# The passage from layer 0 to layer 1 of a two-layer kernel: a sum of expert results on TensorE, layer norm scaled by ScalarE, copies of early attention on ScalarE, and token numbers computed ahead of row numbers

## The chip, the cores and the metric

The kernel runs on one NeuronCore of a Trainium2 chip. The metric is the time of one execution on the device in microseconds (us); the kernel before has a median of 1236.36 us over 3 runs (1234.08 to 1241.92). The engines are called by the names of the profile: PE (TensorE), DVE (VectorE), ACT (ScalarE), POOL (GpSimd) and SP (SyncE, which issues most transfers).

## The reference

Two layers act on 16 x 256 = 4096 tokens of 128 channels in float32. Each layer is a layer norm, a mixer of tokens `s`, an expert network `g`, and a gated sum back into `x`:

```python
x = L0_attn_x
xn = _layernorm(x)
s = _L0_attn_ref(xn, ...)          # gated linear attention, 4 heads, chunks of 64
g = _silu(_L0_ffn_ref(xn, ...))    # 8 experts, the best 2 for each token, weighted
x = x + s * g
xn = _layernorm(x)
s = _L1_attn_ref(xn, ...)          # causal softmax attention, 16 heads of 8 channels
g = _silu(_L1_ffn_ref(xn, ...))    # 16 experts, the best 2, weighted; then an RMS norm
x = x + s * g
```

The change touches the end of layer 0 (`silu` of the two expert results of each token, times `s`, added to `x`), the second layer norm, the routing to experts of both layers, and some copies in the first steps of layer 1's attention.

## The kernel before, in words

**Tiling.** The tokens are 8 blocks of 512 (`BT`), each a tile of 128 partitions x 4 x 128. `xs[b]` holds a block of x, `xns[b]` its norm (the first 128 columns of the tile `xnx`), `xnTs[b]` the transpose of the norm; `s_sbs[b]` is the same memory, taken later for the mixer's result.

**Stages.** Layer 0 starts with norm and routing. Then its experts (`experts0`) run interleaved with its mixer (`gated`, which yields pieces of `decays(b)` and `mixed(b)`). After the last expert, the passage begins: the rest of the mixer for blocks 6 and 7 is interleaved with `combined(b)`, one generator for each block. Then layer 1's attention starts, in pieces, interleaved first with the last steps of `combined` and with layer 1's routing (`route`, lay = 1), later with layer 1's experts (`experts`).

**`combined(b)`** works in four steps. (1) `results` (L439) has SP read both expert results of each token from the DRAM tensor `yd` into the tile `gg` (L444); DVE adds them into `acc` (L767); ACT makes the sigmoid with three activations (L769 to L771); DVE multiplies `acc` by `s` in place (L772). (2) DVE multiplies by the sigmoid (L774), adds into `xs[b]` (L775) and takes mean and variance (L213, L214); ACT makes `rs = exp(-0.5 ln(var + eps))` (L216, L217). (3) DVE scales and shifts x into `xn` in four instructions (L221); PE transposes each quarter (L224); ACT copies the transpose out of PSUM (L225). (4) PE makes the router's logits (L779) and DVE adds their bias (L780). `staged` (L197) starts one block in each tick and moves every live block by one step, oldest first; so a tick holds step 4 of block b-3, step 3 of b-2, step 2 of b-1 and step 1 of b, and then one piece of the mixer. The PSUM tiles of these steps come from the pool `c_ps` of two buffers: L816 while the mixer runs, `pf_` (L1212) after.

**`route`** finds each token's two experts, writes the weighted rows of the norm to DRAM (L285), gives every (token, expert) pair a place in a slot of 128 rows, and inverts this map with one-hot matmuls: in eight rounds DVE makes `ohp` and `hi` (L342, L345), ACT makes `lo` (L346), DVE scales `hi` (L349) and PE adds into `pT` (L351). Then follow the rows for empty slots (L357 to L362), a `yield`, and the copy `tb` of `pT` on ACT (L365) with `row`, `seconds`, `toks` and `rows` on DVE (L367 to L370). At each `yield` of layer 1's route one attention piece is put in (`fill(1)`, L1243). `toks` gives the gather its addresses, `rows` the scatter its own.

**What sets the order.** The passage stands in `manual_schedule` for ACT, PE, DVE and SP: on these, instructions run in the order in which the program makes them. POOL's gathers (`slot_in`, L377) and scatters (`slot_out`, L389) are further ordered by `pooled` and by two helpers: `passed(inst)` (L400) notes an instruction, and `behind(inst)` (L404) makes a transfer wait for the last one that was noted:

```python
def passed(inst):
    reached[:] = [inst.ins.name]

def behind(inst):
    for name in reached:
        tc.add_manual_dep(inst.ins, name, SYNC, reason="spread over other work")
```

After layer 1's route all rows of the first expert batch are gathered at once: `fetch(len(wanted))`, L1248.

**Attention pieces.** `setup(b)` makes kT, qT and v (L886 to L902): `k_part` copies by ACT (L890) and masks by DVE (L892), `q_part` copies qT out of PSUM by DVE (L884). For each tile of 128 queries, scores Sq (L923) give maxima on DVE (L933, L935), `queries` (L985 to L991) makes the shifted queries, scores Sk (L956) go through exponentials on ACT (L963), `weighted` makes `yx` (L1006), DVE copies it to `yt` (L1011), and `normed` transposes (L1018) and divides it into `y` (L1026, L1028). DVE instructions collected in `later` are issued at the next piece. `pS`, `ps` and `pf_` (L1210 to L1212) have two PSUM buffers each.

Of the kernel before, what the change touches and what calls it, by code (L numbers as in the profile page):

```python
# [10 lines left out]
F32 = mybir.dt.float32  # L11
I32 = mybir.dt.int32
BF16 = mybir.dt.bfloat16
AF = mybir.ActivationFunctionType
ALU = mybir.AluOpType
# [43 lines left out]
def two_layer_kernel(  # L59
# [146 lines left out]

    def normed_T(pool, ps, b):

# [7 lines left out]
        nc.scalar.activation(rs, mv[:, :, 1], AF.Ln, bias=eps5)  # L216
        nc.scalar.activation(rs, rs, AF.Exp, scale=-0.5)  # L217
        yield
        pt = ps[0].tile([P, NTL, P], F32, tag=ps[1], name="ptn")
        for t in range(NTL):  # L220
            nc.vector.tensor_scalar(  # L221
                xn[:, t, :], xb[:, t, :], mv[:, t, 0:1], rs[:, t : t + 1], ALU.subtract, ALU.mult
            )
            nc.tensor.transpose(pt[:, t, :], xn[:, t, :], ident)  # L224
# [21 lines left out]
    def route(pool, ps, sc, ne, slt, lay, emap, rm, ptag, tkw):  # L246
# [91 lines left out]
        for c in range(2):  # L338
            for n0 in range(0, NT32, NH):
# [10 lines left out]
                for n in range(NH):  # L350
# [3 lines left out]
                    )  # L354
                yield

        nc.vector.scalar_tensor_tensor(base, cnt, 2.0 * 4096 - 0.5, base, ALU.add, ALU.add)  # L357
# [4 lines left out]
        nc.vector.tensor_tensor(em, em, slotno[:, :slt], ALU.mult)  # L362
        yield
        tb = pool.tile([P, 2, slt], F32, tag="rt_tb", name="tb")
        nc.scalar.copy(tb, pT)  # L365
        row, tok = tb[:, 0, :], tb[:, 1, :]
        nc.vector.scalar_tensor_tensor(row, row, float(P), tok, ALU.mult, ALU.add)  # L367
        nc.vector.tensor_scalar(seconds[lay], row, 4096.0, None, ALU.is_ge)
        nc.vector.scalar_tensor_tensor(toks[lay], seconds[lay], -4096.0, row, ALU.mult, ALU.add)
        nc.vector.tensor_tensor(rows[lay], row, em, ALU.add)  # L370
# [29 lines left out]
    def passed(inst):  # L400

        reached[:] = [inst.ins.name]
# [76 lines left out]
    with ExitStack() as cg:  # L479
# [283 lines left out]
        def combined(b):  # L763

            gg = results(cmb, 0, b)
            acc = cmb.tile([P, NTL, D], F32, tag="acc", name="acc")
            nc.vector.tensor_tensor(acc, gg[:, 0], gg[:, 1], ALU.add)  # L767
            sl = cmb.tile([P, NTL, D], F32, tag="sl", name="sl")
            nc.scalar.activation(sl, acc, AF.Exp, scale=-1.0)  # L769
            nc.scalar.activation(sl, sl, AF.Ln, bias=1.0)  # L770
            nc.scalar.activation(sl, sl, AF.Exp, scale=-1.0)  # L771
            nc.vector.tensor_tensor(acc, acc, s_sbs[b], ALU.mult)  # L772
            yield
            nc.vector.tensor_tensor(sl, sl, acc, ALU.mult)  # L774
            nc.vector.tensor_tensor(xs[b], xs[b], sl, ALU.add)  # L775
            yield from normed_T(cmb, c_ps, b)
            pl = c_ps[0].tile([P, NTL, E1], F32, tag=c_ps[1], name="plg1")
# [47 lines left out]
    with ExitStack() as c1:  # L825
# [41 lines left out]
        def attention():  # L867
# [5 lines left out]
            def setup(b):  # L873
# [6 lines left out]
                def q_part(i):  # L880
                    pq = ps.tile([P, BT], F32, tag="ps", name="pq1")
                    nc.tensor.matmul(pq, wqs[i], xnT, start=True, stop=True)
                    qT[i] = wk_.tile([P, BT], F32, tag=f"qT{i}", name=f"qT{i}")
                    passed(nc.vector.tensor_copy(qT[i], pq))  # L884

# [110 lines left out]
            def weighted(i):  # L996
# [13 lines left out]
                yt = yxs[i] = wk_.tile([P, 4, P], F32, tag="yt", name="yt")  # L1010
                later.append(lambda: passed(nc.vector.tensor_copy(yt, yx)))  # L1011

# [199 lines left out]
        pf_ = c1.enter_context(tc.tile_pool(name="l1pf", bufs=2, space=PSUM))  # L1212
        pieces, ahead, later, done = attention(), [], [], set()

# [20 lines left out]
        with tc.manual_schedule(engines={ET.Activation, ET.PE, ET.DVE, ET.SP}):  # L1235
# [5 lines left out]
            with tc.tile_pool(name="rt1", bufs=1) as rt1:  # L1241
                for _ in route(rt1, pf_, sc1, E1, SLT, 1, emap1, starts(rt1, E1), "pf", {"tag": "pf"}):
                    fill(1)  # L1243
            ccmb.close()
            hp = c1.enter_context(tc.tile_pool(name="l1h", bufs=2))
            batches = [(j0, min(CPB, SLT - j0)) for j0 in range(0, SLT, CPB)]
# [69 lines left out]
```

## Time and profile before

| | us |
|---|---|
| median of 3 runs | 1236.36 |
| lowest and highest run | 1234.08, 1241.92 |
| profiled execution, its own time | 1251.36 |
| its span, first to last instruction | 1249.6 |
| first read of `gg` in the passage (L444) | at 471.9 |
| first DVE sum of results (L767) | at 475.8 |
| mixer of layer 0 done (copy of block 7, L651) | at 564.9 |
| routing of layer 1 begins (L236) | at 591.8 |
| first gather of layer 1 (L377) | at 676.2 |

The profile is one execution. A row of the timeline gives start in the span and duration in us, engine, line of the code, operation, tile written and tiles read, their shape and type, and how many instructions were merged; the bracket at the end is the time for which the engine stood idle before, and the instruction or transfer that released it. A matmul of float32 is two instructions (passes) on PE, so "x4" is two calls. The table of windows gives the busy time of each engine in a stretch, with the number of instructions in parentheses; PEclk is the clock granted to PE as a share of the full one. PEld is the loading of weights into PE, which overlaps its matmuls.

### The profile page before, as it was taken

The numbers are of one execution on the slowest core, as the hardware profiler recorded it, in microseconds if no ns is written. First come the engines' busy times: TensorE is split into PE (matmuls) and PEld (weight loads), VectorE is DVE, ScalarE is ACT, GpSimd is POOL, SyncE is SP. The second block draws the span as 40 slices with busy tenths as digits, with TensorE's granted clock in tenths as the row PEclk, the third lists the DMA queues.
The fourth block names the chain that finished last, engine by engine and source line by source line (L and its number), as shares of the span: only waits on it lengthen the run. The fifth ranks groups of instructions, "written<-read, shape, count | busy, mean of one in ns | idle before, by whom it ended". The sixth has DMA issues, their size and how long they took to land. (4 is left out here: it accounts for less than half of the span.)

```text
span 1249.6 us, 17774 instructions
## 1 busy us (share of the span) xinstructions
PE 910.2 (73%) x6394; PEld 646.3 (52%) x6394; DVE 769.5 (62%) x1442; ACT 588.7 (47%) x1059; POOL 390.2 (31%) x422
## 2 busy tenths in 40 slices
PE   6756478878787773767374887878897889888673
PEld 4334256666566652554142565566565656665342
DVE  5675455646455546736886655756765766675853
ACT  3331267665657462431131455544454655544643
POOL 2000235454455320000103333633652553443120
PEclk9967689899889885677777887988988989899776
DMA  4040248842333202100403030431331333122211
GB/s 112 1 69 1 64 107 211 165 111 72 97 99 106 62 15 88 51 1 1 69 1 129 20 119 18 136 116 33 124 125 48 100 129 117 25 94 66 84 35 34
DMA packets 88415, 95.41 MB, mean 76 GB/s; under 512 B 22228, under 2 KB 64040, under 8 KB 88328
## 3 DMA queue, kind: packets, MB, share of 16 engines
q1 hardware_dynamic: 78632, 74.32, 21.9%
q0 software_dynamic: 9696, 19.97, 6.1%
q8 instruction: 50, 0.82, 0.3%
q14 instruction: 37, 0.30, 0.1%
HBM read 78.03 MB, written 22.51 MB: 80 GB/s over the span
## 5 line engine op out<-in xcount | busy, mean ns | idle before, releaser
L389 POOL DMA_INDIRECT yd<-og,row x150 | 153.8, 1025 | 240.9 <-DVE og L758 116.6
L377 POOL DMA_INDIRECT xg<-xnd,tok x150 | 148.9, 993 | 155.0 <-DVE yT L646 79.7
L956 PE MATMUL Sk<-qm,kT 32*128 32x256 f32 x768 | 129.1, 460 | 43.3 <-ACT pr L963 20.5
L966 POOL TENSOR_SCALAR_AFFINE_SELECT pr<-pr 128x1024 f32<-128x1024 f32 x64 | 72.0, 1125 | 275.7 <-ACT pr L963 275.3
L963 ACT ACTIVATE pr<-Sk 128x1024 f32<-128x1024 f32 x96 | 97.8, 1019 | 96.9 <-PE Sk L956 94.6
L923 PE MATMUL Sq<-km,qT 32*128 32x256 f32 x768 | 132.6, 457 | 12.1 <-DVE mx L933 4.3
L956 PEld LDWEIGHTS Sk<-qm,kT 32*128 32x128 f32 x768 | 76.2, 214 | 61.7 <-ACT pr L963 29.3
L923 PEld LDWEIGHTS Sq<-km,qT 32*128 32x128 f32 x768 | 70.2, 207 | 58.2 <-issue 35.3
L935 DVE TENSOR_REDUCE negm<-Sq 128x8 f32<-128x1024 f32 x64 | 78.0, 1219 | 30.3 <-PE Sk L956 21.7
L721 PEld LDWEIGHTS pf<-xgT,wt 128*128 128x128 f32 x568 | 77.2, 208 | 31.4 <-issue 15.0
L721 PE MATMUL pf<-xgT,wt 128*128 128x128 f32 x568 | 82.9, 294 | 12.0 <-ACT sg L730 6.3
L726 ACT ACTIVATE sg<-pf,nb 128x128 f32<-128x128 f32 x142 | 44.1, 361 | 62.1 <-PE pf L721 61.2
L737 DVE SCALAR_TENSOR_TENSOR gt<-pf,nb,sg 128x128 f32<-128x128 f32 x142 | 42.8, 344 | 47.1 <-ACT sg L730 47.0
L546 PE MATMUL pq<-xnT,sb_wq 128*128 128x512 f32 x64 | 45.4, 850 | 30.0 <-DVE sp L519 28.5
L917 PE MATMUL Sq<-mq,identb 128*128 128x512 bf16 x128 | 42.0, 412 | 16.7 <-DVE negm L935 10.6
L1129 DVE SCALAR_TENSOR_TENSOR z<-pf,z 128x512 f32<-128x512 f32 (+1 forms) x40 | 27.1, 678 | 43.5 <-ACT z L1127 43.5
L1125 ACT ACTIVATE z<-pf 128x512 f32<-128x512 f32 (+1 forms) x40 | 23.7, 593 | 60.9 <-PE pf L1121 60.9
L1173 PE MATMUL pe<-wt,th 128*128 128x128 f32 x316 | 46.7, 309 | 7.0 <-DVE th L1164 7.0
L1173 PEld LDWEIGHTS pe<-wt,th 128*128 128x128 f32 x316 | 43.4, 220 | 14.0 <-issue 10.9
L754 PE MATMUL pe<-sb_wo,gt 128*128 128x128 f32 x284 | 40.1, 300 | 13.0 <-ACT xgT L700 13.0
L754 PEld LDWEIGHTS pe<-sb_wo,gt 128*128 128x128 f32 x284 | 37.2, 210 | 21.5 <-ACT xgT L700 18.1
L351 PE MATMUL pT<-ohj,ohp 128*128 128x142 bf16 (+1 forms) x128 | 14.7, 275 | 45.4 <-DVE ohj L349 45.4
(269 smaller groups left out, 2114.1 us busy)
## 6 DMA issues: line engine op xcount, KB each, us to landing
wt<-bank SPq DMA_DIRECT2D x79, 385.0 KB
wt<-in_w_dram SPq DMA_DIRECT2D x71, 256.0 KB
gg<-yd SPq DMA_DIRECT2D x32, 256.0 KB
xnd<-xnx SPq DMA_DIRECT2D x16, 260.0 KB
xg<-xnd,tok POOLq DMA_INDIRECT x150, 3.4
yd<-og,row POOLq DMA_INDIRECT x150, 2.5
x<-in_x_dram SPq DMA_DIRECT2D x8, 256.0 KB
bank<-in_freq_dram SPq DMA_DIRECT2D x1, 2048.0 KB
```

The lines of the kernel that those rows point to most:

```text
L377: return nc.gpsimd.indirect_dma_start(out=xg[:, i, :], out_offset=None, in_=xnds[lay], in_offset=bass.IndirectOffsetOnAxis(ap=toks[lay][:, ...
L389: give = nc.gpsimd.indirect_dma_start(out=yds[lay], out_offset=bass.IndirectOffsetOnAxis(ap=rows[lay][:, j : j + 1], axis=0), in_=og[:, i, ...
L546: nc.tensor.matmul(pq[:, c], w_[:, h * DK : (h + 1) * DK], xnT, start=True, stop=True)
L721: nc.tensor.matmul(pf[:, c, :], wts[i][:, c * P : (c + 1) * P], xgT[:, i, :], start=True, stop=True)
L726: nc.scalar.activation(sg[:, c, :], pf[:, 2 + c, :], AF.Exp, scale=-1.0, bias=nbs[i][:, 2 + c : 3 + c])
L754: nc.tensor.matmul(pe[:, i, :], gts[i][:, c, :], sb_wo0[:, c, :], start=(c == 0), stop=(c == 1))
L923: nc.tensor.matmul(S[:, c, js, :], qT[part][r, tq], km[r, js, tk], start=not diag, stop=True, skip_group_check=True,)
L935: passed(nc.vector.tensor_reduce(ng, S, AX.X, ALU.max, negate=True))
L956: nc.tensor.matmul(S[:, c, js, :], kT[part][r, tk], qm[r, js, :], start=True, stop=True, skip_group_check=True,)
L963: nc.scalar.activation(pr, S, AF.Exp, scale=scale)
L966: pooled(nc.gpsimd.affine_select(pr_, pr_, pattern=[[0, 8], [1, P]], compare_op=ALU.is_ge, fill=0.0, base=0, channel_multiplier=-1,))
L1173: nc.tensor.matmul(pe[:, i - i0, :], ths[i // 2][:, 2 * (i % 2) + c, :], wts[i][:, 2 * H1 + c * D : 2 * H1 + (c + 1) * D], start=(c == 0), ...
```

## The change

It has four parts. The sum of both results is made by two accumulating matmuls with the identity into a PSUM tile `both`, which ACT and DVE then read. The layer norm of layer 1 alone is scaled by ACT, as `x * rs + nb`, where a new small DVE instruction makes `nb = -mean * rs` behind the statistics. While `early` holds (from the start of layer 1's attention to the end of layer 1's routing), qT and yt are copied by ACT, and these copies are not marked `passed`. In `route` of both layers, `tb`, `row`, `seconds` and `toks` come one `yield` earlier, ahead of the work for empty slots; `rows` stays at the end.

```diff
-    def normed_T(pool, ps, b):
+    def normed_T(pool, ps, b, on_act=False):
...
         nc.scalar.activation(rs, rs, AF.Exp, scale=-0.5)
+        if on_act:
+            nb = pool.tile([P, NTL], F32, tag="nb", name="nb", bufs=3)
+            nc.vector.scalar_tensor_tensor(nb, mv[:, :, 0], -1.0, rs, ALU.mult, ALU.mult)
         yield
         pt = ps[0].tile([P, NTL, P], F32, tag=ps[1], name="ptn")
         for t in range(NTL):
-            nc.vector.tensor_scalar(
-                xn[:, t, :], xb[:, t, :], mv[:, t, 0:1], rs[:, t : t + 1], ALU.subtract, ALU.mult
-            )
+            if on_act:
+                nc.scalar.activation(
+                    xn[:, t, :], xb[:, t, :], AF.Identity, scale=rs[:, t : t + 1], bias=nb[:, t : t + 1]
+                )
+            else:
+                nc.vector.tensor_scalar(
+                    xn[:, t, :], xb[:, t, :], mv[:, t, 0:1], rs[:, t : t + 1], ALU.subtract, ALU.mult
+                )
             nc.tensor.transpose(pt[:, t, :], xn[:, t, :], ident)
...
                 yield
+        tb = pool.tile([P, 2, slt], F32, tag="rt_tb", name="tb")
+        nc.scalar.copy(tb, pT)
+        row, tok = tb[:, 0, :], tb[:, 1, :]
+        nc.vector.scalar_tensor_tensor(row, row, float(P), tok, ALU.mult, ALU.add)
+        nc.vector.tensor_scalar(seconds[lay], row, 4096.0, None, ALU.is_ge)
+        nc.vector.scalar_tensor_tensor(toks[lay], seconds[lay], -4096.0, row, ALU.mult, ALU.add)
+        yield
 
         nc.vector.scalar_tensor_tensor(base, cnt, 2.0 * 4096 - 0.5, base, ALU.add, ALU.add)
...
         nc.vector.tensor_tensor(em, em, slotno[:, :slt], ALU.mult)
-        yield
-        tb = pool.tile([P, 2, slt], F32, tag="rt_tb", name="tb")
-        nc.scalar.copy(tb, pT)
-        row, tok = tb[:, 0, :], tb[:, 1, :]
-        nc.vector.scalar_tensor_tensor(row, row, float(P), tok, ALU.mult, ALU.add)
-        nc.vector.tensor_scalar(seconds[lay], row, 4096.0, None, ALU.is_ge)
-        nc.vector.scalar_tensor_tensor(toks[lay], seconds[lay], -4096.0, row, ALU.mult, ALU.add)
         nc.vector.tensor_tensor(rows[lay], row, em, ALU.add)
         yield
...
             gg = results(cmb, 0, b)
+            both = c_ps[0].tile([P, NTL, D], F32, tag=c_ps[1], name="both")
+            for c in range(2):
+                nc.tensor.matmul(both, ident, gg[:, c], start=(c == 0), stop=(c == 1))
             acc = cmb.tile([P, NTL, D], F32, tag="acc", name="acc")
-            nc.vector.tensor_tensor(acc, gg[:, 0], gg[:, 1], ALU.add)
             sl = cmb.tile([P, NTL, D], F32, tag="sl", name="sl")
-            nc.scalar.activation(sl, acc, AF.Exp, scale=-1.0)
+            nc.scalar.activation(sl, both, AF.Exp, scale=-1.0)
             nc.scalar.activation(sl, sl, AF.Ln, bias=1.0)
             nc.scalar.activation(sl, sl, AF.Exp, scale=-1.0)
-            nc.vector.tensor_tensor(acc, acc, s_sbs[b], ALU.mult)
+            nc.vector.tensor_tensor(acc, both, s_sbs[b], ALU.mult)
             yield
...
-            yield from normed_T(cmb, c_ps, b)
+            yield from normed_T(cmb, c_ps, b, True)
...
-                    passed(nc.vector.tensor_copy(qT[i], pq))
+                    if early:
+                        nc.scalar.copy(qT[i], pq)
+                    else:
+                        passed(nc.vector.tensor_copy(qT[i], pq))
...
-                later.append(lambda: passed(nc.vector.tensor_copy(yt, yx)))
+                later.append(lambda: nc.scalar.copy(yt, yx) if early else passed(nc.vector.tensor_copy(yt, yx)))
...
-        pieces, ahead, later, done = attention(), [], [], set()
+        pieces, ahead, later, done, early = attention(), [], [], set(), [True]
...
             ccmb.close()
+            early.clear()
```

## The prediction

> **What bounds the kernel now.** First the page: no engine is full over the span, so each stage has its own limit.
>
> ```profile
> span 1249.6 us, 17774 instructions
> PE 910.2 (73%) x6394; PEld 646.3 (52%) x6394; DVE 769.5 (62%) x1442; ACT 588.7 (47%) x1059; POOL 390.2 (31%) x422
> ```
>
> The change touches only the passage between the layers. The timeline puts it between 471.85, where the first results of layer 0 are read back, and 676.23, where the first gather of layer 1 starts. So I read that stretch closely. Its first half runs in ticks (one step of each live token block b): here is one, from the `sl` multiply of block 2 to that of block 3.
>
> ```profile
> 497.24 0.68 DVE L774 TENSOR_TENSOR sl<-sl,acc 128x512 f32<-128x512 f32 x1
> 497.64 3.62 PE L546 MATMUL pq<-xnT,sb_wk 128*128 128x512 f32 x4
> 500.29 0.67 DVE L767 TENSOR_TENSOR acc<-gg 128x512 f32<-128x512 f32 x1
> 500.74 0.21 ACT L217 ACTIVATE rs<-rs 128x4 f32<-128x4 f32 x1
> 501.65 0.69 DVE L772 TENSOR_TENSOR acc<-acc,xnT 128x512 f32<-128x512 f32 x1 [0.69 <-ACT sl L769]
> 503.53 1.11 DVE L221 TENSOR_SCALAR xnx<-x,mv,rs 128x128 f32<-128x128 f32 x4
> 504.55 0.68 DVE L774 TENSOR_TENSOR sl<-sl,acc 128x512 f32<-128x512 f32 x1
> ```
>
> DVE is the bound of the tick: 7.31 us without a gap but the 0.69 in which it waits for ScalarE to read `acc` before overwriting it. The table of windows shows TensorE nearly as busy, at half its clock:
>
> ```profile
> core 0: us, PE busy (x) PEld busy (x) DVE busy (x) ACT busy (x) POOL busy (x), PEclk, DMA share, GB/s
> 510.00:515.00 5.00, 4.19 (x8) 2.17 (x9) 4.79 (x17) 1.31 (x4) 0.00 (x0) 0.50 0.30 89
> 525.00:530.00 5.00, 5.00 (x28) 3.37 (x30) 1.90 (x4) 0.06 (x1) 0.00 (x0) 0.50 0.00 0
> ```
>
> From 525 to 565 it is no longer throughput but one chain at a time, for blocks 6 and 7, where ScalarE and DVE wait for each other:
>
> ```profile
> 538.23 1.44 PE L650 MATMUL p_s<-sb_wo,yT 128*128 128x128 f32 x8 [3.46 <-DVE yT L646]
> 540.18 0.63 ACT L769 ACTIVATE sl<-acc 128x512 f32<-128x512 f32 x1
> 542.17 0.69 DVE L774 TENSOR_TENSOR sl<-sl,acc 128x512 f32<-128x512 f32 x1
> 545.92 1.12 DVE L221 TENSOR_SCALAR xnx<-x,mv,rs 128x128 f32<-128x128 f32 x4
> 546.32 1.25 PE L224 MATMUL ptn<-ident,xnx 128*128 128x128 f32 x4 [3.55 <-DVE xnx L221]
> ```
>
> From 590 to 676 routing runs on DVE with attention between; the gathers wait for its last piece:
>
> ```profile
> 611.75 1.02 PE L882 MATMUL pq<-xnT,wqa 128*128 128x512 f32 x2
> 612.81 0.69 DVE L884 COPY qT<-pq 128x512 f32<-128x512 f32 x1 [2.15 <-PE pq L882]
> 613.42 0.68 DVE L315 TENSOR_TENSOR slot<-rk,rt_base 128x512 f32<-128x512 f32 x1
> 676.23 1.01 POOL L377 DMA_INDIRECT xg<-xnd,tok  x1 [8.21 <-DVE y L1028]
> ```
>
> **The change part by part.** A delay or gain that reaches 676 moves everything after it, since the experts' stage starts there with TensorE idle (no matmul from 669 to 681). I walk each chain and sum the shifts at 676.
>
> *Prices.* Adding the two results by TensorE is, for each block, two 128x512 f32 matmuls of two passes each. The nearest rows have the same shape: 3.62 or 3.34 us for four passes at half clock, so 0.85 each and 3.4 a block; 1.02 for two at full clock (L588 at 438.74), so 2.04 a block. Scaling on ScalarE is four 128x128 activations with scale and bias from tensors; the nearest row is L726, 0.63 for two: 1.28 a block, against 1.11 on DVE. The Skill speaks against this move: "Trainium Architecture — The Big Picture", "The five engines, in one table", says that ScalarE is not for simple arithmetic and that DVE is up to about 3 times as fast for an element. That would be 3.3 us a block, an estimate, and another 2 us in each chain below. I take 1.28, since a biased activation of this size stands in the trace. The tiny `nb` on DVE is about 0.2 (L277 has 0.18), but it stands right behind the statistics and needs `rs`: DVE now waits for ScalarE's Ln and Exp (mv done 500.37, rs done 500.95: 0.6). So a tick loses 1.36 (L767 and the wait behind it) and 1.02 (L221) on DVE, and gets 0.8 back: 1.6 net. But TensorE and ScalarE each get more, in an order that crosses: transposes of b-2, sum of b, a piece of layer 0's mixing, logits; exponentials of b, scaling of b-1, copy, `rs`.
>
> *Arrival.* The first sum waits on TensorE's queue for the read-back (475.7), with po (L621) and the next sum queued behind it. TensorE is cold: the second half of its input lands about 475.7, and the sum ends between 477.7 (first half computed while the second lands) and 479.1. The first `sl` multiply goes from 478.49 to 479.8 or 481.2. DVE's shorter tick gives most of it back by the second `sl` (490.44): +1.3 at worst, -0.1 at best. I take +0.5.
>
> *Ticks of blocks 2 to 5 and the tail to ptn of block 5* (before: 6.8, 7.3, 6.8, 7.3, 5.7). At full clock (sum 2.04, pq 2.04, pA 1.06, logits 1.06, transposes 0.6): 5.75 (DVE-bound), 7.2 (transposes wait for scaling until 1.5, then sum, pq, logits), 6.65 (eg and ei, 2.1 on ScalarE, stand ahead of the scaling), 6.75, 5.9: sum -1.65. At half clock (3.4, 3.4, 1.9, 1.7, 1.15) TensorE is the bound: 7.1, 9.0, 9.5, 10.0, 6.2: +7.9. Which clock? The Skill's "TensorE: Matmul & The Clock Gate", "Part 1: The HAM clock gate", says that about 3.4 us of sustained work opens the clock and an idle window of that length closes it; sum and pq in a row would open it, and the ticks would cost -1.65. The row 525:530 above speaks against so simple a rule: fully busy, at 0.50 throughout, much of it with 16-column logits. Yet 484.9 to 488.2, all pq, ends at clock 1.00, and the new passes are of that kind. I weigh the full clock three to one: +0.7.
>
> *526 to 538* is the same work; 0 (to -1.5 with an open clock, +0.5 without).
>
> *Block 6.* L767 lay in the shadow of yT; the sum now stands behind p_s on TensorE, ahead of pA. p_s ends at 539.67, the sum at 542.8 to 543.1 (the clock opened at 542.3), so the exponentials, at 540.18 before, start 2.9 later; `nb` adds 0.2 and scaling on ScalarE 0.1 to 0.3 up to the last transpose. Everything up to p_s of block 7 is behind it: +3.1; open clock +2.3, cold +3.5.
>
> *Block 7.* The same at 564.87, and layer 1's first pk waits behind the sum. Exponentials 2.9 later, scaling 2.5 later; the first scores have to wait for qT on ScalarE behind it. TensorE's pv, which sets the start of the scores, ends 1.0 to 2.7 later; I take +2.0.
>
> *Early copies.* Of four qT and three yt only those count that DVE's chain waits for. The third qT (612.81): `slot` could start with rk at 611.95, -1.4. The fourth (639.35) stands between L937 and L349: -0.6. The last yt (672.83): -0.6. The first two qT, and yt at 626 and 653, lie under TensorE's scores or ScalarE's `lo` (L346): 0, and their cover stays. On ScalarE 0.59 each lies in gaps of 1 to 4 us ahead of L963. If that cover failed, 0.6 each would return. Together -2.7 (-1 to -3.5).
>
> *Tokens ahead of the rows.* The order of instructions shows tb, second and tok ahead of L357-362 on DVE. But a gather is also tied to the last instruction marked `passed`, y (L1028), which stays behind both: 0. In layer 0 the gathers wait for yT (L646) in the same way, and tb on ScalarE fits before L641: 0.
>
> Sum: +0.5 +0.7 +0 +3.1 +2.0 -2.7 +0 = +3.6. The profiled execution took 1251.36 (1249.6 of span and 1.8 around it) and becomes 1255.0. The median of the runs is 1236.36, 15 below the profiled one; with the same shift it becomes 1240.0.
>
> **The rivals.**
> *TensorE stays warm.* The denser work keeps the clock open through the passage. The clock of 1.00 from 645 to 660, with TensorE busy 57 to 83%, speaks for it; its fall to 0.50 after each burst between 490 and 525 against it. Sum +0.5 -1.65 -1.5 +2.3 +1.0 -2.7 = -2.1: 1234.3.
> *TensorE becomes the bound, cold.* At 0.50 throughout, the sum's 3.4 us in each tick makes TensorE the limit: +1.3 +7.9 +0.5 +3.5 +2.7 -2.7 = +13.2: 1249.6, slower by 1.07%. It decides once the ticks alone cost over 7 of the 7.9, that is if hardly a dense burst opens the clock. For it: 505 to 515 at 0.50. Against it: a tick with 6.8 us of wide matmuls in a row has no idle window.
> *Tokens do release the gathers.* If tok alone were the gate, the first gather would start right after it, at about 668 instead of 676.2: -8.3, and the sum -4.7: 1231.7; with a warm TensorE -10.4, 1226.0. Against it: the row of L377 above, which names y. That this part does nothing is my forecast.
>
> **How the numbers follow.** Chances: forecast 0.55, warm 0.25, cold 0.13, tokens 0.07. The likeliest time is 1240.0. The range goes from 1231 (the tokens' case) to 1249.5 (just under the cold case) and leaves out about 0.2: most of the cold case and the far end of the tokens' case. A measurement of this kernel can tell about 1% (12.4 us) from no change. Slower by over 1%: most of the cold case and a little of the forecast's tail, 0.14; faster by over 1% needs 1224, beyond what the tokens and a warm clock give together, so only unseen gains: 0.06; within 1%: 0.80.
>
> **What would show it.** The ticks: distance of the L774 multiplies, 5.7 to 7.2 us with TensorE at 0.7 or more, or 9 and more at 0.50. Block 6: start of the exponentials about 3 us after p_s's end instead of 0.5. Routing: from L236 to the first gather 84.4 before, 81.7 after. The first gather still released by y. The forecast is wrong if the first gather moves by more than 6 us either way, or if the stage behind it changes its own length (573 us from 676.2 to the end) by more than 3.

## The result, and the profile after

The kernel after takes 1247.29 us (median of 20 runs, 1240.65 to 1255.94), the kernel before, beside it on the same chip, 1241.0 (20 runs). The ratio is 1.0049, with a 95% interval from 1.0028 to 1.0071: about 6 us slower, and less than 1%. The median of before lies 5 above that of the three runs shown ahead of the prediction, so what compares with the forecast is the shift: +3.6 was predicted, +3.5 to +8.8 is the interval (0.28% to 0.71% of 1241.0). All ratios in this document leave out the slow executions and are not the quotient of the two medians. The profiled execution of after took 1252.05 (before: 1251.36). Its layer 0 is 4.0 shorter (the first results are read at 467.8 instead of 471.9), with the same code there except the order of the routing's last piece, and that piece is no shorter: from the start of the last gate multiply ahead of it (L593 of before) to layer 0's first gather 6.77 us instead of 6.63. In e4 below, whose layer 0 has the code of before again, the first read is at 466.4. So the 4.0 is a difference between executions, and all passage times below are counted from the first read of `gg`.

The head of the profile page of after:

```profile
span 1250.3 us, 17847 instructions
PE 924.7 (74%) x6426; PEld 647.3 (52%) x6426; DVE 755.7 (60%) x1403; ACT 604.2 (48%) x1098; POOL 392.0 (31%) x422
```

DVE has 13.8 us less, ACT and PE have about 15 more each. That is what the change says, and it tells nothing of the time. The passage does. Landmarks, in us from the first read (one profile each):

| | before | after | shift |
|---|---|---|---|
| `sl` multiply of block 0 | 6.6 | 8.9 | +2.3 |
| of block 1 | 18.6 | 19.9 | +1.3 |
| of block 2 | 25.4 | 25.5 | +0.1 |
| of block 3 | 32.7 | 33.8 | +1.1 |
| of block 5 | 46.8 | 47.5 | +0.7 |
| p_s of block 6 | 66.4 | 67.9 | +1.5 |
| `sl` of block 6 | 70.3 | 74.5 | +4.2 |
| p_s of block 7 | 91.0 | 96.0 | +5.0 |
| `sl` of block 7 | 95.8 | 102.5 | +6.7 |
| routing begins (L236 of before, L244 of after) | 120.0 | 127.9 | +7.9 |
| first gather of layer 1 | 204.4 | 208.9 | +4.5 |
| from there to the end | 573.4 | 573.5 | +0.1 |

The first results arrive. In the timeline of after the sum is the first thing that waits for them:

```profile
470.97 3.75 PE L776 MATMUL both<-gg,ident 128*128 128x512 f32 x4 [8.56 <-DMA gg<-yd]
475.39 0.69 DVE L782 TENSOR_TENSOR acc<-both,xnT 128x512 f32<-128x512 f32 x1 [12.81 <-ACT sl L779]
```

The sum takes 3.75 (DVE's add took 0.69), and DVE's product still waits for ACT's exponential, although `acc` is now a new tile that ACT never reads.

One tick of after, from the `sl` multiply of block 2 to that of block 3:

```profile
493.20 1.63 ACT L225 ACTIVATE xnx<-x,nb,rs 128x128 f32<-128x128 f32 x4
493.35 0.68 DVE L784 TENSOR_TENSOR sl<-sl,acc 128x512 f32<-128x512 f32 x1
493.74 1.48 PE L232 MATMUL ptn<-ident,xnx 128*128 128x128 f32 x4 [2.07 <-ACT xnx L225]
495.05 2.94 PE L776 MATMUL both<-gg,ident 128*128 128x512 f32 x4
...
497.09 0.16 DVE L220 SCALAR_TENSOR_TENSOR nb<-mv,rs 128x4 f32<-128x4 f32 x1 [0.60 <-ACT rs L217]
497.78 2.58 PE L554 MATMUL pq<-xnT,sb_wk 128*128 128x512 f32 x4
...
498.03 0.60 ACT L779 ACTIVATE sl<-both 128x512 f32<-128x512 f32 x1 [0.97 <-PE both L776]
...
498.65 0.69 DVE L782 TENSOR_TENSOR acc<-both,xnT 128x512 f32<-128x512 f32 x1 [1.40 <-ACT sl L779]
...
500.39 1.23 DVE L558 TENSOR_TENSOR kk<-pq,ei 128x1024 f32<-128x1024 f32 x1 [1.05 <-PE pq L554]
...
501.67 0.68 DVE L784 TENSOR_TENSOR sl<-sl,acc 128x512 f32<-128x512 f32 x1
```

Read it as one chain: ACT's scaling paces the transposes, behind them on TensorE's queue stands the sum, behind the sum pq, behind pq DVE's kk, and behind kk the next `sl`. DVE was the bound of the tick with a gap of 0.69; now it has gaps of 0.60, 1.40 and 1.05 in this stretch, and the tick takes 8.32 instead of 7.31. It is the longest of the four: from block 1 to block 5 they take 5.57, 8.32, 7.08 and 6.61, and 6.80, 7.31, 6.80 and 7.31 before.

The windows over the ticks, 30 us each (columns as in the prediction); first before:

```profile
469.00:499.00 30.00, 9.59 (x30) 6.24 (x31) 19.62 (x44) 8.40 (x16) 1.73 (x4) 0.58 0.31 92
499.00:529.00 30.00, 22.98 (x83) 16.40 (x81) 22.45 (x67) 12.51 (x25) 0.00 (x0) 0.61 0.18 53
```

The same for after:

```profile
465.00:495.00 30.00, 16.67 (x64) 8.27 (x65) 15.94 (x35) 10.02 (x22) 1.72 (x4) 0.72 0.31 92
495.00:525.00 30.00, 25.74 (x91) 14.45 (x91) 16.20 (x52) 19.10 (x42) 0.00 (x0) 0.80 0.18 53
```

The clock opens, 0.58 and 0.61 to 0.72 and 0.80, and DVE's load in the second window falls from 22.45 to 16.20. Yet from the `sl` of block 1 to that of block 5 it takes 27.6 us instead of 28.2, and 28.3 to 28.4 in e4, e7 and e11 below, which have the same instructions there.

Block 6 of after, in the timeline:

```profile
535.77 1.18 PE L658 MATMUL p_s<-sb_wo,yT 128*128 128x128 f32 x8 [3.47 <-DVE yT L654]
536.75 3.57 PE L776 MATMUL both<-gg,ident 128*128 128x512 f32 x4
540.35 0.60 ACT L779 ACTIVATE sl<-both 128x512 f32<-128x512 f32 x1 [2.77 <-PE both L776]
542.31 0.69 DVE L784 TENSOR_TENSOR sl<-sl,acc 128x512 f32<-128x512 f32 x1
...
546.25 1.65 ACT L225 ACTIVATE xnx<-x,nb,rs 128x128 f32<-128x128 f32 x4 [0.23 <-DVE nb L220]
546.80 1.63 PE L232 MATMUL ptn<-ident,xnx 128*128 128x128 f32 x4 [4.70 <-ACT xnx L225]
```

p_s ends at 536.95 and the exponential starts at 540.35, 3.4 later; before it was 0.5. Ahead of p_s, TensorE stood idle for 3.47, waiting for yT, while the two results that it was to add had long been there (the last reads of `gg` were issued at 512.4).

Block 7, the same timeline further on:

```profile
565.58 2.81 PE L776 MATMUL both<-gg,ident 128*128 128x512 f32 x4
...
569.05 0.69 DVE L782 TENSOR_TENSOR acc<-both,xnT 128x512 f32<-128x512 f32 x1 [1.25 <-ACT sl L779]
...
569.80 1.12 PE L901 MATMUL pk<-xnT,wka 128*128 128x512 f32 x2 [1.42 <-DVE acc L782]
```

Layer 1's first pk reads nothing of block 7's `acc`, but waits 1.42 for it, probably because its buffer of PSUM had been that of `both`. Where DVE makes block 7's sum (before, e1, e6), pk waits 1.33 for DVE's `mrow` instead.

Routing, in the timeline of after:

```profile
616.50 0.69 DVE L323 TENSOR_TENSOR slot<-rk,rt_base 128x512 f32<-128x512 f32 x1 [1.39 <-PE rk L320]
...
676.76 1.01 POOL L385 DMA_INDIRECT xg<-xnd,tok  x1 [7.83 <-DVE y L1041]
```

DVE reaches `slot` before `rk` is there, which no copy of qT delays any more. The gather is still released by y, though tok was done at 669.5.

### The profile page after: what moved, and what is told of

Read it like the earlier page. It is cut to its first block, busy times and chain, and to the rows that moved or that the text cites. A ratio compares the mean times of both kernels' runs of the same rounds, so it can differ in the third digit from the quotient of the medians.

```text
span 1250.3 us, 17847 instructions
## 1 busy us (share of the span) xinstructions
PE 924.7 (74%) x6426; PEld 647.3 (52%) x6426; DVE 755.7 (60%) x1403; ACT 604.2 (48%) x1098; POOL 392.0 (31%) x422
## 3 DMA queue, kind: packets, MB, share of 16 engines
q1 hardware_dynamic: 78632, 74.32, 21.6%
## 5 line engine op out<-in xcount | busy, mean ns | idle before, releaser
L385 POOL DMA_INDIRECT xg<-xnd,tok x150 | 149.4, 996 | 154.3 <-DMA wt<-in_w_dram 79.7
L936 PEld LDWEIGHTS Sq<-km,qT 32*128 32x128 f32 x768 | 70.3, 207 | 57.0 <-issue 36.1
L948 DVE TENSOR_REDUCE negm<-Sq 128x8 f32<-128x1024 f32 x64 | 78.0, 1219 | 30.7 <-PE Sk L969 21.1
L930 PE MATMUL Sq<-mq,identb 128*128 128x512 bf16 x128 | 44.2, 431 | 16.0 <-DVE negm L948 9.4
L554 PE MATMUL pq<-xnT,sb_wq 128*128 128x512 f32 x64 | 42.6, 801 | 18.1 <-DVE sp L527 16.7
L1138 ACT ACTIVATE z<-pf 128x512 f32<-128x512 f32 (+1 forms) x40 | 23.7, 593 | 62.1 <-PE pf L1134 61.2
L1186 PEld LDWEIGHTS pe<-wt,th 128*128 128x128 f32 x316 | 43.9, 222 | 13.2 <-issue 10.2
L762 PEld LDWEIGHTS pe<-sb_wo,gt 128*128 128x128 f32 x284 | 37.9, 213 | 22.3 <-ACT xgT L708 19.3
L1160 PEld LDWEIGHTS pm<-xgT,wt 128*128 128x128 f32 x316 | 44.5, 222 | 6.5 <-issue 6.2
```

Source lines behind the costliest of these rows:

```text
L385: return nc.gpsimd.indirect_dma_start(out=xg[:, i, :], out_offset=None, in_=xnds[lay], in_offset=bass.IndirectOffsetOnAxis(ap=toks[lay][:, ...
L762: nc.tensor.matmul(pe[:, i, :], gts[i][:, c, :], sb_wo0[:, c, :], start=(c == 0), stop=(c == 1))
L930: nc.tensor.matmul(S[:, c], identb, mq, start=True, stop=False, skip_group_check=True)
L936: nc.tensor.matmul(S[:, c, js, :], qT[part][r, tq], km[r, js, tk], start=not diag, stop=True, skip_group_check=True,)
L948: passed(nc.vector.tensor_reduce(ng, S, AX.X, ALU.max, negate=True))
L1160: nc.tensor.matmul(pm[:, k, :], wts[i][:, H1 + c * P : H1 + (c + 1) * P], xgTs[i // 4][:, i % 4, :], start=True, stop=True,)
```

## The experiments

The theory after the result: TensorE's sum costs time where it stands in an in-order queue on the only live chain (arrival, blocks 6 and 7), the scaling on ACT costs a little, the copies gain, the tokens do nothing. The rival: the sum is harmless, and the loss comes from ACT's scaling and from the waits that it brings to DVE. The first four runs are after with one part undone. In the experiments, "passage" is the time from the first read of `gg` to layer 1's first gather (before 204.4, after 208.9), and the number behind it is the routing stretch within it, from the beginning of routing to that gather (before 84.4, after 81.0). All ratios are to the kernel before, on the same chip. The first four ran where before takes 1240.5. The others ran on two other chips, where it takes 1304.7 (e5 to e8) and 1312.3 (e9 to e12): there the stages on both sides of the passage are longer (the first read is at 503 to 519, the stage behind the gather takes 598 to 603), so only ratios and the inner times of the passage are set against each other. No profile of the kernel before was taken on these two chips, and one profile stands for each run. How far passages differ without an edit shows in two pairs: e5 comes to routing 1.7 before the kernel before (118.3 and 120.0), e7 3.2 before after (124.7 and 127.9), each with the same instructions up to there. So a passage of e5 to e12 is set against the first six profiles only where the distance at the edit's own place shows the same.

### e1: the sum back on DVE

```diff
-            both = c_ps[0].tile([P, NTL, D], F32, tag=c_ps[1], name="both")
-            for c in range(2):
-                nc.tensor.matmul(both, ident, gg[:, c], start=(c == 0), stop=(c == 1))
             acc = cmb.tile([P, NTL, D], F32, tag="acc", name="acc")
+            nc.vector.tensor_tensor(acc, gg[:, 0], gg[:, 1], ALU.add)
+            both = acc
```

> The changed kernel with the sum of the two results back on DVE; scaling on ScalarE, early copies and token order stay changed. Measured in the profile as the passage, from the first read of the results to the first gather of layer 1: 204.4 us before, 209.0 after the change. Theory A (the sum costs, because it stands in TensorE's queue on the chains of blocks 0, 6 and 7): the passage falls to about 203, and the time is 5 to 6 us under the changed kernel's, about 0 to 1 us under the kernel before. Theory B (the scaling on ScalarE with the wait for nb costs): the passage stays at 207 or more.

Measured: 1240.28 us, ratio 0.9984 [0.9952, 1.0016]; passage 200.2 (80.6). The `sl` multiplies stand at 6.5, 18.7, 25.2, 32.3, 39.6, 46.7, 69.5 and 95.5: those of blocks 6 and 7 come 5.0 and 7.0 earlier than in after, those of the ticks 0.3 to 1.5 (block 0: 2.4). Without the sum the loss is gone, and 8.7 of the passage with it. The clock in the two windows falls back to 0.60 and 0.56, and the ticks hardly notice: 28.0 from block 1 to block 5, against 27.6. So it is the sum that opens the clock, and the sum and the open clock together bring next to nothing in the ticks.

### e2: the scaling back on DVE

```diff
-            yield from normed_T(cmb, c_ps, b, True)
+            yield from normed_T(cmb, c_ps, b)
```

> The changed kernel with the layer norm scaled by DVE again and without nb; the sum on TensorE, early copies and token order stay. Theory A: passage 207 to 208, only 1 to 2 us better than the changed kernel, since the sum's delays stay. Theory B: about 204, and the whole loss is gone.

Measured: 1246.39 us, ratio 1.0034 [1.0005, 1.0064]; passage 206.9 (80.9). The `sl` of blocks 6 and 7 are at 72.7 and 100.3, 1.8 and 2.2 earlier than in after, of which 1.8 was there at p_s of block 6 (66.1). But those 1.8 lie between `sl` of block 5 and p_s of block 6 (18.6 instead of 20.4), a distance that is 19.6 in before and 17.2 in e5 with the same instructions. The ticks are steadier: 27.4 from block 1 to block 5 here, as in the other runs with the sum on TensorE and the scaling on DVE (e6, e10 and e12: 27.4), and 27.6 to 28.4 with both moved (after, e3, e4, e7 and e11). So the scaling on ACT costs at most about 2 of the passage, and the time doesn't show it, since the intervals of the two ratios overlap. The rival can't carry the loss.

### e3: the copies back on DVE

```diff
-        pieces, ahead, later, done, early = attention(), [], [], set(), [True]
+        pieces, ahead, later, done, early = attention(), [], [], set(), []
```

> The changed kernel with all early copies of qT and yt back on DVE. By the prediction's step the copies gain 2.7 us, by the profile after up to 3.5 in routing: the passage grows from 209.0 to 211.7 to 212.5. If they lie in DVE's idle time, it stays at 209.

Measured: 1253.69 us, ratio 1.0110 [1.0074, 1.0146]; passage 208.8 (82.8). The passage missed the 211.7 that was expected: routing is 1.9 longer, but the first half is 2.0 shorter in this profile (p_s of blocks 6 and 7 at 65.0 and 94.0), where the edit moves nothing. The time says more than the passage: 0.6% above after, about 7.6 us, of which the routing stretch shows 1.9. In its one profile the stage behind the gather took 578.5 instead of 573.5; e1, e2 and e4, which have after's code there, took 576.7, 570.5 and 570.4. Whether the rest is the edit or this one execution stays open.

### e4: the tokens back behind the rows

```diff
-        tb = pool.tile([P, 2, slt], F32, tag="rt_tb", name="tb")
...
-        nc.vector.scalar_tensor_tensor(toks[lay], seconds[lay], -4096.0, row, ALU.mult, ALU.add)
-        yield
...
         nc.vector.tensor_tensor(em, em, slotno[:, :slt], ALU.mult)
+        yield
+        tb = pool.tile([P, 2, slt], F32, tag="rt_tb", name="tb")
...
+        nc.vector.scalar_tensor_tensor(toks[lay], seconds[lay], -4096.0, row, ALU.mult, ALU.add)
         nc.vector.tensor_tensor(rows[lay], row, em, ALU.add)
```

> The changed kernel with tb, row, seconds and toks after the work for empty slots again. By the prediction this part does nothing: passage 209.0 within 0.5, first gather released by y, and layer 0's first gather no later than its own yT. If the early tokens gain something, the passage grows by up to 4, or the stretch before it by as much.

Measured: 1247.27 us, ratio 1.0046 [1.0016, 1.0075]; passage 209.2 (80.7). tok starts at 206.9 instead of 201.4 and the first gather is where it was (209.2 and 208.9). The part does nothing that these runs can show.

### e5: the copies alone

Before, with the copies on ACT as the only change. Against after:

```diff
-            both = c_ps[0].tile([P, NTL, D], F32, tag=c_ps[1], name="both")
...
+            nc.vector.tensor_tensor(acc, gg[:, 0], gg[:, 1], ALU.add)
+            both = acc
...
-            yield from normed_T(cmb, c_ps, b, True)
+            yield from normed_T(cmb, c_ps, b)
```

and the tokens as in e4.

> The kernel before with the early copies on ScalarE alone. If the copies are worth what the stretch from the first step of routing (the maxima of the logits) to the first gather says, 84.4 us before and 81.0 after, the passage is 201.0 and the time 3 us (0.25%) under the kernel before. If the 7.6 us that their removal cost in e3 are theirs, 7 us (0.6%) under it. Beside e1 (passage 200.2), which differs by the scaling and the token order, it tells what the scaling on ScalarE is worth with the sum on DVE: nothing, if both are within 1 us.

Measured: 1303.51 us, ratio 0.9995 [0.9960, 1.0030]; passage 199.0 (80.7). Routing is 3.7 shorter than in before; the other 1.7 of the passage lie ahead of routing, where the code is that of before. In the time that isn't resolved: the interval holds both 0 and the 0.28% that 3.7 us would be.

### e6: the sum on TensorE in the ticks only

```diff
+            if 0 < b < 6:
+                both = c_ps[0].tile([P, NTL, D], F32, tag=c_ps[1], name="both")
+                for c in range(2):
+                    nc.tensor.matmul(both, ident, gg[:, c], start=(c == 0), stop=(c == 1))
+            else:
+                nc.vector.tensor_tensor(acc, gg[:, 0], gg[:, 1], ALU.add)
+                both = acc
...
-            yield from normed_T(cmb, c_ps, b, True)
+            yield from normed_T(cmb, c_ps, b)
```

> The changed kernel with the scaling on DVE, and the sum on TensorE for blocks 1 to 5 alone, on DVE for blocks 0, 6 and 7. Theory A (the sum costs where it stands on a chain, not in the ticks): against e2 (206.9) the passage falls by 5 to 7 us, to 200 to 202. If TensorE is also the bound of the ticks, the sixth sl multiply comes over 1 us later than before (46.8 us from the first read) and the passage stays over 203.

Measured: 1304.16 us, ratio 0.9970 [0.9934, 1.0006]; passage 195.5 (80.2), 11.4 shorter than e2, which has the sum in all blocks, and below the 200 to 202 expected. What the edit's own places show is 6.6: `sl` of block 0 comes 2.2 earlier, from p_s to `sl` it takes 3.9 instead of 6.5 in block 6 and 4.8 instead of 6.5 in block 7. Of the rest, some 3 lie between `sl` of block 6 and p_s of block 7 (17.8 instead of 21.1). That distance goes with the clock: with the sums of both blocks on DVE, p_s of block 7 comes 24.6 to 25.8 after that of block 6 in before, e1 and e5, at a mean clock of 0.70 to 0.72, and 21.6 to 22.3 in e6, e8 and e10, at 0.81 to 0.83. Why the clock differs there is not shown. The `sl` of block 5 is at 46.0 (before 46.8), and the ticks from block 1 to block 5 take 27.4, as in e2, e10 and e12; with sum and scaling on DVE they take 28.2 to 28.3 (before, e5, e8). So the sum does no harm in the ticks, and with the scaling on DVE it brings 0.8 us, too little for the times to show. The harm is in blocks 0, 6 and 7.

### e7: the first gather not tied to y

```diff
-    def fetch(k):
+    def fetch(k, tied=True):
...
-            behind(inst)
+            if tied:
+                behind(inst)
...
-            fetch(len(wanted))
+            fetch(len(wanted), False)
```

> The changed kernel with the first batch of layer 1's gathers no longer tied to the last passed instruction (y). By the prediction's reading y is what holds the early tokens back. If it alone does, the first gather starts right after tok, some 7 us earlier (passage 202). If the memory of the gathered tile, which routing uses until its last instruction, holds it too, it starts with the end of rows, 2 us earlier (207), and the time gains 0 to 2 us.

Measured: 1308.25 us, ratio 1.0027 [0.9998, 1.0055]; passage 204.5 (79.8); of the 4.4 that it is shorter than after's, 3.2 lie ahead of routing, where nothing was edited. The timeline of e7 names the next gate:

```profile
704.37 0.24 DVE L369 SCALAR_TENSOR_TENSOR tok<-second,tb 128x79 int32<-128x79 f32 x1
...
709.68 0.24 DVE L378 TENSOR_TENSOR row<-tb,rt_em 128x79 int32<-128x79 f32 x1
...
710.71 1.01 POOL L385 DMA_INDIRECT xg<-xnd,tok  x1 [6.69 <-DVE row L378]
```

Without the tie the gather starts 1.2 sooner, measured from the beginning of routing, and not 8: tok has been there for six microseconds, but now the end of `row` holds it, on which the gathered tile's memory seems to depend. Two gates stood one behind the other, and taking away the first shows the second. That memory wasn't moved, so the 5 us between tok and row are not shown to be winnable.

### e8: copies and tokens, the gather untied, sum and scaling on DVE

```diff
-            both = c_ps[0].tile([P, NTL, D], F32, tag=c_ps[1], name="both")
...
+            both = acc
...
-            yield from normed_T(cmb, c_ps, b, True)
+            yield from normed_T(cmb, c_ps, b)
...
-            fetch(len(wanted))
+            fetch(len(wanted), False)
```

> Early copies on ScalarE, tokens ahead and the first gathers not tied to y; sum and scaling on DVE as before. If the parts add up: passage 199 to 201, the time 3 to 6 us under the kernel before (0.25 to 0.5%). If the stage behind gives the gain back, the passage is short and the time the same as before.

Measured: 1300.01 us, ratio 0.9963 [0.9926, 0.9999]; passage 194.6 (79.1), below the 199 to 201 expected; from `sl` of block 5 to p_s of block 7 it takes 39.6 instead of 44.2 before with the same instructions, so the passage overstates the edit. Faster than before, by little.

### e9: `nb` behind the yield

DVE's wait for `rs` ahead of `nb` (0.60 in the tick above) was to be taken off by issuing `nb` a step later.

```diff
         nc.scalar.activation(rs, rs, AF.Exp, scale=-0.5)
+        yield
         if on_act:
             nb = pool.tile([P, NTL], F32, tag="nb", name="nb", bufs=3)
             nc.vector.scalar_tensor_tensor(nb, mv[:, :, 0], -1.0, rs, ALU.mult, ALU.mult)
-        yield
```

> The changed kernel with nb made one step later, at the head of the step that scales: DVE no longer stands 0.6 us behind the statistics for ScalarE's rs. If this wait costs the ticks, they shrink by up to 0.6 each, the sixth sl multiply comes at 44.5 to 47 us from the first read (47.5 in the changed kernel) and the passage falls by 1 to 3. If the ticks are bound by TensorE and ScalarE, nothing moves beyond 0.5, and blocks 6 and 7 gain at most 0.2 each.

Measured: 1319.2 us, ratio 1.0060 [1.0027, 1.0092]; passage 209.4. The expectation missed: the ticks grow, the `sl` multiplies are at 19.7, 27.3, 35.5, 43.5 and 52.2 for blocks 1 to 5 (32.5 in all instead of 27.6). The timeline of e9 shows where `nb` is now:

```profile
557.00 1.88 PE L554 MATMUL pq<-xnT,sb_wq 128*128 128x512 f32 x4
...
558.92 1.22 DVE L556 SCALAR_TENSOR_TENSOR qg<-pq,eg 128x1024 f32<-128x1024 f32 x1 [0.40 <-PE pq L554]
...
560.19 0.15 DVE L221 SCALAR_TENSOR_TENSOR nb<-mv,rs 128x4 f32<-128x4 f32 x1
...
560.38 1.65 ACT L225 ACTIVATE xnx<-x,nb,rs 128x128 f32<-128x128 f32 x4 [1.25 <-DVE nb L221]
```

It lies behind `qg` on DVE (in other ticks behind kk), the mixer's work of the tick before, and ACT's scaling, which starts the chain of the next tick, waits for it: 1.25 here, 0.24 and 0.53 in two other ticks; in one tick ACT was busy until after `nb` and no wait shows. The short wait was cheap; the place at the head of the step was not.

### e10: e6 with the gather untied

The edits of e6 and e7 together.

```diff
+            if 0 < b < 6:
...
-            yield from normed_T(cmb, c_ps, b, True)
+            yield from normed_T(cmb, c_ps, b)
...
+            fetch(len(wanted), False)
```

> The sum on TensorE for blocks 1 to 5 alone, scaling on DVE, early copies on ScalarE, tokens ahead, first gathers not tied to y. If the parts of e6 and e7 add up: passage 1 to 2 us under e6's (195.5), and the time 3 to 6 us under the kernel before (0.25 to 0.5%). If it beats e8 (0.9963), the sum in the ticks is worth something.

Measured: 1307.06 us, ratio 0.9966 [0.9936, 0.9997]; passage 191.1 (79.1). As fast as e8 (0.9963), which has no sum on TensorE at all. Of the 4.4 that its passage is shorter than e6's, 1.1 lie in routing and 3.2 between `sl` of block 5 and p_s of block 6, where both have the same instructions.

### e11: the same instructions, the sums of blocks 6 and 7 issued earlier

If it is the place in the queue and not the work, the same sum must be nearly free in the gap in which TensorE waits for yT, ahead of p_s.

```diff
+        boths = {}
...
+        def summed(b):
             gg = results(cmb, 0, b)
             both = c_ps[0].tile([P, NTL, D], F32, tag=c_ps[1], name="both")
             for c in range(2):
                 nc.tensor.matmul(both, ident, gg[:, c], start=(c == 0), stop=(c == 1))
+            return both
...
+            both = boths.pop(b, None) or summed(b)
```

and in the mixer, after the multiply that makes `yT`:

```diff
+            if b >= 6:
+                boths[b] = summed(b)
```

> The changed kernel with the same instructions, but the sums of blocks 6 and 7 issued one piece earlier on TensorE, between pss and p_s, where it stands idle for 3.5 us for DVE's yT. If the loss is the place in the queue, the exponentials of block 6 start within 0.7 us after p_s ends (3.4 in the changed kernel), and the passage falls by 4 to 6, to 203 to 205. If the loss is TensorE's added work itself, or the clock, it stays at 207 or more.

Measured: 1311.45 us, ratio 0.9999 [0.9969, 1.0029]; passage 202.2 (80.9), 6.7 shorter than after and 3.4 earlier at the beginning of routing than e7, the run on another chip with after's code up to there. p_s of blocks 6 and 7 are at 68.0 and 93.0, their `sl` at 71.6 and 97.0 (after: 67.9, 96.0, 74.5, 102.5). The timeline of e11 at block 6:

```profile
570.41 1.88 PE L779 MATMUL both<-gg,ident 128*128 128x512 f32 x4
...
574.04 1.13 PE L660 MATMUL p_s<-sb_wo,yT 128*128 128x128 f32 x8 [1.75 <-DVE yT L654]
...
575.69 0.60 ACT L787 ACTIVATE sl<-both 128x512 f32<-128x512 f32 x1
...
577.65 0.69 DVE L792 TENSOR_TENSOR sl<-sl,acc 128x512 f32<-128x512 f32 x1
```

The sum ends 1.75 before p_s can start, and the exponential comes 0.5 after p_s's end, as in before. This is the run that settles it: nothing was removed, only moved within TensorE's queue. The distance from p_s to `sl` shows it whatever the chip and the clock. With the sum behind p_s (after, e2, e4, e7 and e9) it is 6.5 in block 6 and 6.3 to 6.5 in block 7 (e3: 7.4 and 6.5); with the sum ahead of p_s (e11 and e12) 3.6 and 4.1; with the sum on DVE 3.6 to 4.6 and 4.4 to 4.8. So the place costs 2.9 and 2.4 us here, 5.4 in all; the 6.7 of the passage also hold differences between profiles.

### e12: e11, with the scaling on DVE and the gather untied

```diff
+                boths[b] = summed(b)
...
-            yield from normed_T(cmb, c_ps, b, True)
+            yield from normed_T(cmb, c_ps, b)
...
+            fetch(len(wanted), False)
```

> e11 with the scaling on DVE and the first gathers not tied to y: all sums on TensorE, none on a chain but block 0's. If only the place of the sum was wrong: passage 200 to 202, within 1.5 us of e10 but for block 0 (1.4). If the early sum only shifts the loss, 205 or more.

Measured: 1305.1 us, ratio 0.9919 [0.9886, 0.9952]; passage 194.2 (79.7), below the expected passage. It beats both kernels by its ratio; 0.81% of 1312.3 is 10.6 us. How large the gain is stays less certain than that: the medians are 7.2 apart, and the profile is of the longest of its executions (1317.48), in which the first read comes only at 519.1, and 4.2 of the 10.2 by which its passage is shorter than that of before lie between `sl` of block 5 and p_s of block 6 (15.4 instead of 19.6), a stretch that is as short in e10 without any sum in it. Against e8 and e10 the intervals overlap, so that the early sum itself is worth more than a sum on DVE is not shown.

## Why the prediction was right, point by point

**The size and the side.** +3.6 was forecast; the passage is 4.5 longer and the runs 6 (3.5 to 8.8). Two misses cancel in part: up to the beginning of routing +6.3 was forecast and +7.9 measured, in routing -2.7 and -3.4. The early copies' own terms (-1.4, -0.6 and -0.6) add up to -2.6, not -2.7. The time of the forecast (1240.0) and its range hung on a median of three runs 5 below that of twenty.

**Arrival: mis-sized.** Forecast +0.5 at the second `sl`, between -0.1 and +1.3; measured +1.3, the far end. The sum at the cold clock (0.50 from 470 to 474.8) took 3.75 instead of 3.4. And the wait of 0.69 behind ACT's exponential, which the prediction took as gone because `acc` is no longer overwritten in place, stayed: L782 waits for ACT in all eight blocks, with 23.7 us of idle time ahead of it in all (12.8 of it at the arrival and 5.4 in block 6, where most is waiting for the sum itself).

**Ticks: right in sum, wrong in why.** Forecast +0.7 up to the last transposes of block 5 and 0 from there to 538; measured -0.6 from block 1 to block 5 (+0.1 to +0.2 in e4, e7 and e11) and +0.8 from there to p_s of block 6. The warm rival had the clock right: 0.72 and 0.80. "TensorE: Matmul & The Clock Gate", "Part 1: The HAM clock gate", of the Trainium skill says that about 3.4 us of sustained work opens the clock; the windows agree so far that the clock rose with the sum and fell without it (e1: 0.60 and 0.56). The row 525:530 of the prediction does not show that narrow work keeps the clock down: 2.7 of its 5 us are pq, which is 128x512 and ran from 524.12 to 527.74 at 0.50, and the clock opened only at 532. But the rival's gain (-1.65) didn't come. The step that failed is the tick at full clock, "7.2 (transposes wait for scaling until 1.5, then sum, pq, logits)": the chain was right, its terms were too short. Scaling and transposes lasted until 1.9 after the `sl`, the sum 2.94 instead of 2.04, pq 2.58 instead of 2.04: the clock was open for part of the tick only (0.79 over the tick, 0.63 from 495 to 498), and it took 8.32 (8.0 to 9.1 in e3, e4, e7 and e11). The other three took 5.6, 7.1 and 6.6, near the 5.75, 6.65 and 6.75 of the forecast.

**Scaling on ACT: mis-sized, small.** Four take 1.63 to 1.65 instead of the forecast 1.28; on DVE 1.11. The row of L726 (0.63 for two) has its scale as a constant and reads PSUM; this one has scale and bias as tensors. The rule of "Trainium Architecture — The Big Picture", "The five engines, in one table" (DVE up to about 3 times as fast) would give an estimated 3.3; measured is 1.5 times. Undoing it (e2) gains 2.0 of the passage, 1.8 of it in a distance that varies as much without an edit.

**Block 6: right.** Forecast: exponentials 2.9 later, +3.1 up to p_s of block 7. Measured: 3.4 after p_s's end instead of 0.5, which is 2.9 later, and +3.5. The 2.9 stands in every run with the sum behind p_s. Part of the 3.5 may be the clock, since the same distance varies by 4 between profiles of kernels with the same work there (e6).

**Block 7: right in kind, mis-sized.** Forecast +2.0, measured +2.9 (+1.7 to the `sl`, +1.2 from there to the beginning of routing). What wasn't in the sum: pk's wait of 1.42 for L782, probably for the PSUM buffer that `both` held. The slower scaling is no part of the 1.2: from `sl` of block 7 to routing e1, with the scaling on ACT, takes 24.0 (before 24.2), and e2, with it on DVE, 25.7 (after 25.4).

**Copies and routing: right.** Forecast -2.7 (-1 to -3.5), measured -3.4 in after and -3.7 alone (e5). In e3 it is 1.9 the other way. No cost on ACT shows in routing: the cover named (gaps of 1 to 4 us) held.

**Tokens: right.** 0 was forecast, because y releases the gather. y releases it in after, e4 shows no difference, and e7 shows that even without y the next gate is 1.2 away and not 8.3, as that rival had it.

**The stage behind** keeps its length: 573.5 and 573.4. That they agree to 0.1 is luck: profiles of e1, e2 and e4, with after's code there, give 570.4 to 576.7.

**Left open:** why e3 is 7.6 us above after when its passage isn't; whether the 0.8 us that the sum brings in the ticks reaches the time (e6 and e10 against e8); and what of the 6 us in the time, beyond the 4.5 of the passage, is real.

## What to carry to other kernels

Work that is moved to an idle engine costs by its place in that engine's in-order queue: 2.8 to 3.6 us of sum behind p_s, on the only live chain, delayed the next `sl` by 2.9 and 2.4 us, and the same instructions one piece earlier, in a gap of that engine, cost nothing there. An open clock and an unloaded DVE are worth only what the chain of the tick lets through, so write that chain down across all engines before you count an engine's savings. And when a transfer has several gates, moving the input that isn't the last of them gains nothing: look for the second gate before you remove the first.

## What the runs showed that was not expected

- Two engines that only read the same PSUM tile stand one behind the other in this program: DVE's product of `both` starts when ACT's exponential of `both` has ended, 0.02 to 0.04 later in all eight blocks and in every other run with the sum on TensorE. No data goes from the one to the other; why the wait is there was not tried.
- The scaling on ACT with scale and bias as tensors takes 1.63 for four 128x128 tiles, 1.5 times DVE's 1.11, and TensorE's transposes follow at that pace (mostly 1.48 to 1.63 instead of 1.13 to 1.25).
- The two other chips take 5 to 6% longer for the same kernel (1304.7 and 1312.3 against 1240.5). In the profiles of e5 to e12 this lies outside the passage: the first read is 31 to 37 us later than in before (in e12 47) and the stage behind the gather 24 to 29 us longer. Why is not shown.
- Profiles of kernels with the same work between p_s of block 6 and p_s of block 7 differ by 4 us there (21.6 to 25.8). Differences of a few microseconds in one profile are safe only where the edit's own place shows them.
